# A four-layer convolution chain: the first spectral layer's rows back along w, moved into the work on both sides of their stage

## The chip, the cores and the metric

The kernel runs on one core of a Trainium2 chip. The metric is the device time of one execution in microseconds, as a median of several runs. Of the kernel before, three runs gave 3878.82, 3879.38 and 3880.02 us, a median of 3879.38 us. The profile is of one execution with a span of 3876.6 us, and all times in the trace count from the start of that span.

## The reference

The input is an image of 48 x 48 positions with 768 channels in float32. Four layers follow each other: an attention block with an MLP (layer 0), a spectral layer (1), a scan (2) and a second spectral layer (3). The change touches the end of layer 1 and the beginning of layer 2.

```
# layer 1 (and 3): FFT over h and w, a small complex MLP on 8 blocks of 96 channels, FFT back, plus x
xs = fft2(x) over (h, w), half of w kept: 25 columns
o1 = relu(xs @ w1 + b1); o2 = o1 @ w2 + b2          # complex, by blocks
x = irfft2(softshrink(o2)) + x
# layer 2: projections of every position, then 12 steps of a diffusion
B, C = silu(x @ W_B + ..), silu(x @ W_C + ..)       # 256 wide each
X, alpha, theta, gamma = x @ W_X, W_dec, W_th, W_lam # 4, 64, 32 and 1 wide
for i in range(12):
    inj = rope(B, theta * (i + 1)) * X
    H = alpha * depthwise3x3(H) + (1 - gamma) * alpha * prev + gamma * inj
```

The inverse FFT is done in two parts: back along h, and then back along w. The second part is what this study calls the rows back.

## The kernel before

The spectrum of layer 1 lies in DRAM in two tensors, `yu[0]` and `yu[1]`, for the two halves of 384 channels each. `spectrum_mix` reads it in items: for each half (first 1, then 0), each group of 5 columns of the spectrum and each block of 96 channels. An item goes through four stages: FFT along h (`s_fft_h`, L1420), first layer (`s_mlp1`, L1434 to L1445), second layer and softshrink (`s_mlp2`, L1455 to L1461), and FFT back along h (`s_ifft_h`, L1470 to L1477). The stages are staggered over steps: in one step the FFT of item i stands beside the last stage of item i - 4. After 40 items there are four more steps that only drain what is under way. A group of 5 columns is stored to `yu` when its four blocks are done. After each step a hook is called (`beside(step)`); in the kernel before it makes the last forward FFT rows in steps 1 and 4, and loads the scan's weights `wsc` in step 8.

Then the rows back (`afno_first`, L1549 to L1558). For each half and each of 6 groups of 8 image rows, `load_spectrum` reads a tile `gt` of 672 KB from `yu` (three buffers). For each of three tiles of 128 channels, four products with `gt` as weights (100 x 128) and the small matrix `iw` (100 x 96) as moving operand fill 384 columns of a PSUM bank, which `Evac` copies in turn on ScalarE (L57) and VectorE (L59) into `x2T`, the whole image with channels on partitions. That is 144 products and 36 copies.

Then the scan (`scan_phase`). Its left-side tiles are set up (memsets on GpSimd, L1045 and L1047; four PSUM tiles `pss` of two banks, cleared on VectorE, L1043). The projections (L1082) run over 24 tiles of two image rows. A tile takes 12 products of 112 positions: six for 357 columns and six for 256, one for each 128 channels of x. VectorE adds the bias while it empties the two banks (L1084). Three tiles make a q, and for each of 8 q a chain on VectorE and ScalarE follows: silu, sigmoid, sines and cosines for the rope, and the start values of the recurrence (`H`, `s0`, `s1`). Then the steps of the diffusion begin (L1172 on).

The order of instructions on each engine is not that of the source. A scheduler places them by its own costs and by what they depend on, so instructions of different stages are interleaved where their data allows it. At run time each engine runs its own list in order, and waits at an instruction whose semaphores are not yet there. DMAs of these stages are issued from one queue (SP), in order too.

Of the kernel before, what the change touches and what calls it, by code (L numbers as in the profile page):

```python
# [2 lines left out]

# [8 lines left out]
F32 = mybir.dt.float32  # L12
# [7 lines left out]
P = 128  # L20
G = 48
T = G * G
C = 768
NC = C // P
NT = T // P
NH, HD = 12, 64
FF = 4 * C
NF = FF // P
TB = 384
NTB = T // TB  # L30
# [6 lines left out]
NB, BS = 8, 96  # L37
KW = G // 2 + 1
KC = 5
YR = 112  # L40
NKC = KW // KC
# [955 lines left out]
    return r, a  # L997


def scan_phase(tc, ident, w, w_close, wts, xT, xT_close, c_d, cr_d, out_open):  # L1000

# [18 lines left out]
    with tc.tile_pool(name="sc_s", bufs=1, side="left") as sp:  # L1022
# [9 lines left out]
        with (  # L1032
# [6 lines left out]
            bands0 = stp.tile([P, GC, 4, G], F32, tag="bands0", name="bands0")  # L1039
            nc.sync.dma_start(bands0, bands_d[:, :GC])  # L1040
            pss = [pm.tile([P, 2, 512], F32, tag=f"c{i}", name=f"c{i}") for i in range(4)]
            for ps in pss:
                V.memset(ps, 0.0)  # L1043
            top = slice(96, P)
            GP.memset(H, 0.0)  # L1045
# [2 lines left out]
            with (  # L1048
# [10 lines left out]
                def temp(shape, tag, q, bufs=1):  # L1059
                    return tp.tile([P, *shape], F32, tag=tag, name=f"{tag}_{q}", bufs=bufs)[:K]  # L1060
# [8 lines left out]
                def over_r(v, n):  # L1069
                    return v.unsqueeze(2).to_broadcast([K, n, RR, R4])  # L1070

                for q in range(NQ):
                    prs = slice(q * R4, (q + 1) * R4)
                    za = temp([NA, R4], "za", q, 2)
                    g = temp([NCR, R4], "g", q, 2)
                    for t in range(R4):
                        tok = (q * R4 + t) * P
                        ps = pss[(q * R4 + t) % 4]
                        parts = ((za, 0, NA), (g, NA, NCR))
                        for i, (z, c0, n) in enumerate(parts):  # L1080
                            for cc in range(NC):
                                nc.tensor.matmul(ps[:K, i, :n], lhsT=xT[:, cc, tok : tok + K], rhs=w[:, cc, c0 : c0 + n], start=cc == 0, stop=cc == NC - 1)  # L1082
                        for i, (z, c0, n) in enumerate(parts):
                            V.tensor_tensor(z[:, :, t], ps[:K, i, :n], bias[:K, c0 : c0 + n], ALU.add)  # L1084
                    g3 = g.rearrange("p (n r) t -> p n r t", r=RR)
                    c, x = za[:, :NCR, :], za[:, NA - 1 - RR : NA - 1, :]
                    thz = za[:, NCR + NN : NCR + NN + NM, :]
                    alq = al[:K, :, prs]
                    ga = temp([1, R4], "ga", q)
                    for t in (g, x):  # L1090
                        nc.scalar.activation(t, t, AF.Silu)
                    th = temp([NM * R4], "th", q)
                    V.tensor_copy(th, thz.rearrange("p m t -> p (m t)"))
                    cs = sincos(th, q, "t1")
                    V.tensor_scalar(th, th, float(ITERS), None, ALU.mult)
                    cs12 = sincos(th, q, "t12")
                    nc.scalar.activation(c, c, AF.Silu)
                    nc.scalar.activation(ga, za[:, NA - 1 : NA, :], AF.Sigmoid)
                    nc.scalar.activation(alq, za[:, NCR : NCR + NN, :], AF.Sigmoid)
                    nc.sync.dma_start(c_d[:K, q, :NCR], c)  # L1100
                    nc.sync.dma_start(c_d[:K, q, NCR:].rearrange("p (s m) t -> p s m t", s=2), cs12)
                    c1q = c1[:K, :, prs]
                    V.tensor_scalar(c1q, cs[:, 0], 2.0, None, ALU.mult)

                    def by_gamma(out, in_):
                        for t in range(R4):
                            nc.scalar.mul(out[:, :, t], in_[:, :, t], ga[:, 0, t : t + 1])


                    om = temp([1, R4], "om", q)  # L1110
                    V.tensor_scalar(om, ga, -1.0, 1.0, ALU.mult, ALU.add)
                    be = temp([NN, R4], "be", q)
                    V.tensor_tensor(be, alq, om.to_broadcast([K, NN, R4]), ALU.mult)
                    bc = temp([NN, R4], "bc", q)
                    gc = temp([NM, R4], "gc", q)
                    V.tensor_tensor(gc, c1q, ga.to_broadcast([K, NM, R4]), ALU.mult)
                    for j in range(2):
                        ms = slice(j * NM, (j + 1) * NM)
                        V.tensor_tensor(bc[:, ms], be[:, ms], gc, ALU.add)
                    ac = temp([NN, R4], "ac", q)  # L1120
                    V.tensor_tensor(ac, alq, cb[:K].unsqueeze(2).to_broadcast([K, NN, R4]), ALU.mult)

                    V.tensor_tensor(g.rearrange("p (n r) t -> p n (r t)", r=RR), g.rearrange("p (n r) t -> p n (r t)", r=RR), x.rearrange("p r t -> p (r t)").unsqueeze(1).to_broadcast([K, NN, RR * R4]), ALU.mult)
                    i0 = temp([NCR, R4], "i0", q)
                    i03 = i0.rearrange("p (n r) t -> p n r t", r=RR)
                    m = [temp([NM, RR, R4], f"m{j}", q) for j in range(2)]
                    for op in turn(V, i0, g, over_r(cs[:, 0], NM), over_r(cs[:, 1], NM), m):
                        op()

                    V.tensor_tensor(H[:K, :, :, 1 + q * R4 : 1 + (q + 1) * R4], i03, over_r(ac, NN), ALU.add)  # L1130
                    flat = lambda v: v.rearrange("p n r t -> p (n r) t")

                    u = temp([NCR, R4], "u", q)
                    by_gamma(u, i0)
                    t0 = s0[:K, :, :, prs]
                    V.tensor_tensor(t0, g3, over_r(be, NN), ALU.mult)
                    V.tensor_tensor(flat(t0), flat(t0), u, ALU.add)
                    u = temp([NCR, R4], "u", f"{q}_1")
                    by_gamma(u, g)
                    t1 = s1[:K, :, :, prs]  # L1140
                    V.tensor_tensor(t1, i03, over_r(bc, NN), ALU.mult)
                    V.tensor_tensor(flat(t1), flat(t1), u, ALU.subtract)  # L1142
            w_close()
            xT_close()
            wo, bo = out_weights()
            with (
                tc.tile_pool(name="sc_h", bufs=1, side="right") as hp,
# [115 lines left out]
def block_kernel(ctx: ExitStack, tc: tile.TileContext, a: dict):  # L1263
# [41 lines left out]
    def opened(name, shape, side):  # L1305
        stack = ExitStack()
        pool = stack.enter_context(tc.tile_pool(name=name, bufs=1, side=side))
        return pool.tile(shape, F32, tag=name, name=name), stack.close
# [21 lines left out]
    follow_in = lambda *args: afno_follow(nc, xa_d, a["fw2"], yu, todo, *args)  # L1330
    mlp_phase(tc, ident, w1s_d, a["mlp_b1"], a["mlp_w2"], w2s_d, a["mlp_b2"], a["ln2_g"], a["ln2_b"], xr_d, xa_d, follow_in)

    x2T, x2T_close = opened("x2T", [P, NC, G * HD], "right")
    wsc, wsc_close = opened("wsc", [P, NC, a["W_scan"].shape[1]], "right")
    afno_first(tc, a, yu, x2T, follow_in, lambda: nc.sync.dma_start(wsc, a["W_scan"].rearrange("(c p) n -> p c n", p=P)))

    closes = []

# [5 lines left out]
    wts = [a[k] for k in ("b_scan", "bias_scan", "conv_b", "bands", "W_out", "b_out")]  # L1344
    c_d = dram.tile([P, 8, NN * RR + 2 * NM, 3], F32, tag="c_d", name="c_d")
    cr_d = dram.tile([P, 8, NN * RR, 3], F32, tag="cr_d", name="cr_d")
    x3 = scan_phase(tc, ident, wsc, wsc_close, wts, x2T, x2T_close, c_d, cr_d, out_open)
    afno_second(tc, a, x3, yu)
    for close in reversed(closes):
        close()  # L1350
# [138 lines left out]
def load_spectrum(nc, pool, yu, half, g, name, bufs):  # L1489
    gt = pool.tile([YR, 4, TB], F32, tag="gt", name=f"{name}_gt_{half}_{g}", bufs=bufs)  # L1490
    nc.sync.dma_start(gt, yu[half][:, 4 * g : 4 * g + 4, :])
    return gt
# [33 lines left out]
    return follow  # L1526


def afno_first(tc, a, yu, x2T, follow_in, load_next):

    nc = tc.nc
    ev = Evac(nc)
    x2v = x2T.rearrange("p c (h w) -> p c h w", w=HD)
    nc.gpsimd.memset(x2v[:, :, :, G:], 0.0)
    with (
        tc.tile_pool(name="f1_g", bufs=1, side="right") as gp,  # L1540
        tc.tile_pool(name="f1_p", bufs=8, space=PSUM) as pm,
    ):

        def psum(tag):
            return pm.tile([P, 512], F32, tag="m", name=f"f1_{tag}")

        iw = gp.tile([4 * KW, BS], F32, tag="iw", name="f1_iw")
        follow = follow_in(gp, 1)
        spectrum_mix(tc, "f1", a, "L1", yu, psum, True, "left", (1, 0), lambda step: follow(psum) if step in (1, 4) else load_next() if step == 8 else None)  # L1549
        nc.sync.dma_start(iw, a["iw"])  # L1550
        for half in (1, 0):
            for g in range(NTB):
                gt = load_spectrum(nc, gp, yu, half, g, "f1", 3)
                for ct in range(NC // 2):
                    ps = psum(f"w_{half}_{g}_{ct}")
                    for i in range(4):
                        nc.tensor.matmul(ps[:, i * BS : (i + 1) * BS], lhsT=gt[: 4 * KW, i, ct * P : (ct + 1) * P], rhs=iw, start=True, stop=True)
                    ev(x2v[:, half * NC // 2 + ct, 8 * g : 8 * g + 8, :G], ps[:, :TB].rearrange("p (h w) -> p h w", w=G))  # L1558


def afno_second(tc, a, x3, yu):
# [145 lines left out]
```

## Time and profile before

| stretch | from, us | to, us | what TensorE does |
|---|---|---|---|
| spectrum mix, layer 1 | 2850 | 3049.3 | f_x, f_o, f_z, f_u; clock 1.00 from 2866 to 3049 |
| rows back along w | 3049.3 | 3110.5 | f_w, 144 products |
| wait for the first bank | 3110.5 | 3112.5 | nothing |
| projections of the scan | 3112.5 | 3264.1 | c, 288 products |
| rest of the chain of the last q | 3264.1 | 3275.6 | nothing |
| diffusion steps | 3275.6 | 3519 | c from H and bands |

In the profile, the page's first part gives each engine's busy time. A line of a list of stretches has the stretch, its length, then for each engine the busy time and in parentheses the number of records, the granted clock of TensorE as a share of full speed, the busy share of the DMA engines and their rate. A product of float32 operands shows as two records of weight load and two of matmul. In the lines of single instructions, the brackets say how long the engine was idle before and what ended that.

### The profile page before, as it was taken

Reading aid. Unit: us, or ns where it says so; the run is one execution under the profiler, and the core shown is the slowest. Engines: PE = TensorE matmul, PEld = TensorE weight load, DVE = VectorE, ACT = ScalarE, POOL = GpSimd, SP = SyncE. Lnnn points to the kernel's source line nnn. Section 1 sums busy time; section 2 is a strip of 40 time slices with the busy share of each in tenths; the row PEclk is TensorE's granted clock in tenths of the full one; section 3 lists DMA queues with packets and bytes.
Section 4 is the critical chain, followed back from the end, with each engine's and each line's share of the span. In section 5 each row is a group of like instructions: output and inputs, shape, how many; then the busy total and the mean of one; then the engine's idle time right before and its main releaser. Section 6 shows DMA issues by size and latency. Waiting matters only on the chain. (4 is left out here: it accounts for less than half of the span.)

```text
span 3876.6 us, 54460 instructions
## 1 busy us (share of the span) xinstructions
PE 3761.5 (97%) x22018; PEld 2285.7 (59%) x22018; DVE 2059.0 (53%) x3185; ACT 1141.9 (29%) x1907; POOL 658.4 (17%) x496
## 2 busy tenths in 40 slices
PE   8999989999999999998999999999999998999998
PEld 4666544444444444455555555555568866996685
DVE  6655456666666666555425333232335367995355
ACT  1322244444444444421310120021023246223341
POOL 3101011111111111024000000000023301981131
PEclk9999989999999999999999999999999799999999
DMA  7656563424232322134334434433454302110444
GB/s 257 210 187 197 173 183 112 127 92 133 84 110 83 105 87 76 36 95 161 123 105 155 150 107 124 147 122 108 132 139 110 96 24 93 40 32 22 146 108 159
DMA packets 266810, 460.43 MB, mean 119 GB/s; under 512 B 32989, under 2 KB 219349, under 8 KB 260055
## 3 DMA queue, kind: packets, MB, share of 16 engines
q1 hardware_dynamic: 256919, 436.23, 36.3%
q10 hardware_dynamic: 9632, 20.65, 1.4%
q8 instruction: 175, 2.87, 0.3%
q14 instruction: 84, 0.69, 0.1%
HBM read 318.49 MB, written 138.31 MB: 118 GB/s over the span
## 5 line engine op out<-in xcount | busy, mean ns | idle before, releaser
L576 DVE TENSOR_TENSOR acc<-acc,p 128x768 f32<-128x768 f32 x576 | 582.8, 1012 | 354.9 <-ACT p L568 316.5
L568 ACT ACTIVATE p<-s 128x768 f32<-128x768 f32 x648 | 478.5, 812 | 692.7 <-PE s L566 580.5
L929 PE MATMUL p<-w,h 128*128 128x384 f32 x1512 | 492.7, 486 | 0.0
L558 PE MATMUL s<-qt,kv 64*128 64x384 f32 x2592 | 478.5, 501 | 9.1 <-ACT p L568 7.4
L587 PE MATMUL av<-p,kv 128*64 128x384 f32 x2592 | 464.5, 493 | 0.0
L929 PEld LDWEIGHTS p<-w,h 128*128 128x128 f32 x1512 | 286.1, 190 | 196.9
L558 PEld LDWEIGHTS s<-qt,kv 64*128 64x128 f32 x2592 | 233.1, 187 | 249.9 <-ACT p L568 116.0
L587 PEld LDWEIGHTS av<-p,kv 128*64 128x64 f32 x2592 | 170.0, 136 | 225.2 <-issue 215.8
L866 PE MATMUL p<-x2nT,w 128*128 128x384 f32 x864 | 294.0, 490 | 3.1 <-issue 3.1
L294 PE MATMUL qk<-xnT,wqk 128*128 128x384 f32 x756 | 252.5, 491 | 5.2 <-DMA wqk<-wqk_d 5.2
L1172 PE MATMUL c<-H,bands 128*48 128x96 f32 x5632 | 242.8, 247 | 12.1 <-issue 11.5
L566 PE MATMUL s<-bt,oneh 120*128 120x384 bf16 x1296 | 248.3, 328 | 0.0
L1172 PEld LDWEIGHTS c<-H,bands 128*48 128x48 f32 x5632 | 234.2, 123 | 20.9 <-issue 11.9
L866 PEld LDWEIGHTS p<-x2nT,w 128*128 128x128 f32 x864 | 165.4, 192 | 119.1 <-issue 6.0
L866 PE MATMUL p<-xT,w 128*128 128x384 f32 x648 | 220.8, 486 | 0.0
L566 PEld LDWEIGHTS <-oneh 120*128 120x128 bf16 x1296 | 109.1, 98 | 174.3 <-issue 115.1
L294 PEld LDWEIGHTS qk<-xnT,wqk 128*128 128x128 f32 x756 | 144.6, 193 | 99.9 <-issue 8.5
L905 POOL TENSOR_TENSOR rr<-rr,ml_b 128x1152 f32<-128x1152 f32 x12 | 33.5, 2788 | 954.4 <-DMA rr<-xr_d 660.8
L861 ACT ACTIVATE h<-h,ml_b 128x384 f32<-128x384 f32 x144 | 88.3, 614 | 346.6 <-DVE h L881 174.3
L1180 POOL TENSOR_TENSOR t<-s,c 128x768 f32<-128x768 f32 x80 | 144.8, 1836 | 214.3 <-DVE s L1142 203.8
L866 PEld LDWEIGHTS p<-xT,w 128*128 128x128 f32 x648 | 123.1, 190 | 85.9
L1082 PE MATMUL c<-wsc,x2T 128*112 128x357 f32 (+1 forms) x576 | 151.6, 426 | 2.0 <-DVE c L1043 2.0
(314 smaller groups left out, 4778.7 us busy)
## 6 DMA issues: line engine op xcount, KB each, us to landing
w<-w1s_d SPq DMA_DIRECT2D x36, 768.0 KB
w<-w2s_d SPq DMA_DIRECT2D x36, 768.0 KB
bt<-rh_d SPq DMA_DIRECT2D x144, 162.0 KB
w<-w1s_d SPq DMA_DIRECT2D x36, 576.0 KB
w<-in_mlp_w_dram SPq DMA_DIRECT2D x27, 768.0 KB
wqk<-wqk_d SPq DMA_DIRECT2D x12, 1344.0 KB
yu<-f_ys SPq DMA_DIRECT2D x24, 672.0 KB
f_gt<-yu SPq DMA_DIRECT2D x24, 672.0 KB
```

Source lines behind the costliest of these rows:

```text
L294: nc.tensor.matmul(p[:, :TB], lhsT=w[:, n, c, :], rhs=ops[sb][n][:, c, :], start=c == 0, stop=c == NC2 - 1)
L558: nc.tensor.matmul(ps[:, s, :QB], lhsT=keys[pr % 2][rows, kt * P : (kt + 1) * P], rhs=qbs[qc % 2][0][rows], start=True, stop=False)
L566: nc.tensor.matmul(ps[:, s, :QB], lhsT=oneh[:NBR, b % 3, :], rhs=qbs[qc % 2][1][:NBR, s, b // 3, j, :], start=False, stop=True)
L568: nc.scalar.activation(p, ps[:, :, :QB], AF.Exp)
L576: nc.vector.tensor_tensor(probs[c], probs[c], p, ALU.add)
L587: nc.tensor.matmul(avs[c][rows, :QB], lhsT=vals[pr % 2][:, kt, rows], rhs=p[:, s, :], start=kt == 0, stop=kt == NT - 1)
L861: nc.scalar.activation(h, h, AF.Gelu, bias=b1c[:, k : k + 1])
L866: nc.tensor.matmul(p[:, :TB], lhsT=w[n][:, c, :], rhs=rhs[n][:, c, :], start=c == 0, stop=c == NC2 - 1)
L929: nc.tensor.matmul(ps[t][:, :TB], lhsT=hs[left, f][:, t * P : (t + 1) * P], rhs=wt[:, f % KW2, :], start=f == 0, stop=f == NF2 - 1)
L1082: nc.tensor.matmul(ps[:K, i, :n], lhsT=xT[:, cc, tok : tok + K], rhs=w[:, cc, c0 : c0 + n], start=cc == 0, stop=cc == NC - 1)
L1172: nc.tensor.matmul(ps[r0 : r0 + G, k // 4, cols], lhsT=bands[:, n - GC, i, :] if gr else bands0[:, n, i, :], rhs=H[:, n, :, d : d + NPR], ...
L1180: GP.tensor_tensor(t, sc[:, ch], c1[:, m0 : m0 + GC].unsqueeze(2).to_broadcast([P, GC, RR, NPR]), ALU.mult)
```

## The change

The rows back lose their stage. Those of half 1, whose spectrum is complete when the mix turns to half 0, are made beside the last items: tiles of `gt` are loaded in four of the last steps, one group of 8 image rows follows each of the four draining steps, and two more come after them. They go into `xh`, which holds only this half of the channels. Those of half 0 are made inside the scan's projections: group 0 ahead of the first tile, and each further group two tiles ahead of the four tiles that read it. They go into one of two small homes (`x2_0`, `x2_1`), each for 8 image rows. For these products the fourth of the PSUM tiles is used, one bank for each group of 384 columns in turn, so the projections have three tiles in place of four. A projection sums the six channel tiles in reversed order, so that those from `xh` come first.

The tiles `gt` (now four buffers), `iw` and the two homes lie in a pool that lives until the projections end. The loads of the scan's biases find room earlier; the scheduler puts them, and the sum of the two biases, into the early mix. `gc` shares the buffer of `th`. The purpose is to take a stage away in which only one kind of work is done, and to lay its work beside others.

```diff
 def scan_phase(...)
-            for ps in pss:
+            for ps in pss[:3]:
                 V.memset(ps, 0.0)
...
+                turn_of = itertools.cycle(range(2))
+                banks = lambda tag: pss[3][:, next(turn_of), :]
+                xs = [rows_back(0, banks)]
                 for q in range(NQ):
...
                     for t in range(R4):
-                        tok = (q * R4 + t) * P
-                        ps = pss[(q * R4 + t) % 4]
+                        pr = q * R4 + t
+                        if pr % 4 == 2 and pr + 4 < NPR:
+                            xs.append(rows_back(pr // 4 + 1, banks))
+                        x_of = lambda cc: (xs[pr // 4], cc, pr % 4 * P) if cc < NC // 2 else (xh, cc - NC // 2, pr * P)
+                        ps = pss[pr % 3]
...
-                            for cc in range(NC):
-                                nc.tensor.matmul(ps[:K, i, :n], lhsT=xT[:, cc, tok : tok + K], rhs=w[:, cc, c0 : c0 + n], start=cc == 0, stop=cc == NC - 1)
+                            for cc in reversed(range(NC)):
+                                v, c, tok = x_of(cc)
+                                nc.tensor.matmul(ps[:K, i, :n], lhsT=v[:, c, tok : tok + K], rhs=w[:, cc, c0 : c0 + n], start=cc == NC - 1, stop=cc == 0)
...
-                    gc = temp([NM, R4], "gc", q)
+                    gc = temp([NM * R4], "th", f"{q}_g").rearrange("p (m t) -> p m t", t=R4)
 def afno_first(...)
+    iw = rp.tile([4 * KW, BS], F32, tag="iw", name="f1_iw")
+    homes = [rp.tile([P, HC, 8 * HD], F32, tag=f"x2{i}", name=f"x2_{i}") for i in range(2)]
...
+    def load(half, g):
+        gts[half, g] = load_spectrum(nc, rp, yu, half, g, "f1", 4)
+
+    def back(half, g, dst, psum):
+        gt = gts.pop((half, g))
+        for ct in range(HC):
+            ps = psum(f"w_{half}_{g}_{ct}")
+            for i in range(4):
+                nc.tensor.matmul(ps[:, i * BS : (i + 1) * BS], lhsT=gt[: 4 * KW, i, ct * P : (ct + 1) * P], rhs=iw, start=True, stop=True)
+            ev(in_rows(dst)[:, ct, :, :G], ps[:, :TB].rearrange("p (h w) -> p h w", w=G))
...
-        nc.sync.dma_start(iw, a["iw"])
-        for half in (1, 0):
-            for g in range(NTB):
-                gt = load_spectrum(nc, gp, yu, half, g, "f1", 3)
-                for ct in range(NC // 2):
-                    ps = psum(f"w_{half}_{g}_{ct}")
-                    for i in range(4):
-                        nc.tensor.matmul(ps[:, i * BS : (i + 1) * BS], lhsT=gt[: 4 * KW, i, ct * P : (ct + 1) * P], rhs=iw, start=True, stop=True)
-                    ev(x2v[:, half * NC // 2 + ct, 8 * g : 8 * g + 8, :G], ps[:, :TB].rearrange("p (h w) -> p h w", w=G))
+        def first_back(g):
+            back(1, g, xh[:, :, 8 * g * HD : 8 * (g + 1) * HD], psum)
+            if g + 4 < NTB:
+                load(1, g + 4)
+
+        def beside(step):
+            last = 2 * NKC * (NB // 2)
...
+            elif last - 12 <= step < last - 4 and step % 2 == 0:
+                load(1, (step - last + 12) // 2)
+            elif step >= last:
+                first_back(step - last)
+
+        spectrum_mix(tc, "f1", a, "L1", yu, psum, True, "left", (1, 0), beside)
+        for g in range(4, NTB):
+            first_back(g)
+            load(0, g - 4)
+
+    def rows_back(g, banks):
+        if g + 2 < NTB:
+            load(0, g + 2)
+        back(0, g, homes[g % 2], banks)
+        return homes[g % 2]
```

More of the change, by code (lines that the diff above doesn't have):

```diff
@@ L1 @@
+import itertools
 import math
@@ L997, in reduce_angle, with scan_phase @@
     return r, a
-def scan_phase(tc, ident, w, w_close, wts, xT, xT_close, c_d, cr_d, out_open):
+def scan_phase(tc, ident, w, wts, rows_back, xh, x_close, c_d, cr_d, out_open):
     nc = tc.nc
@@ L1142, in scan_phase @@
                     V.tensor_tensor(flat(t1), flat(t1), u, ALU.subtract)
-            w_close()
-            xT_close()
+            x_close()
             wo, bo = out_weights()
@@ L1331, in block_kernel @@
     mlp_phase(tc, ident, w1s_d, a["mlp_b1"], a["mlp_w2"], w2s_d, a["mlp_b2"], a["ln2_g"], a["ln2_b"], xr_d, xa_d, follow_in)
-    x2T, x2T_close = opened("x2T", [P, NC, G * HD], "right")
+    xh, xh_close = opened("xh", [P, NC // 2, G * HD], "right")
     wsc, wsc_close = opened("wsc", [P, NC, a["W_scan"].shape[1]], "right")
-    afno_first(tc, a, yu, x2T, follow_in, lambda: nc.sync.dma_start(wsc, a["W_scan"].rearrange("(c p) n -> p c n", p=P)))
+    rp_stack = ExitStack()
+    rp = rp_stack.enter_context(tc.tile_pool(name="f1_w", bufs=1, side="right"))
+    rows_back = afno_first(tc, a, yu, xh, rp, follow_in, lambda: nc.sync.dma_start(wsc, a["W_scan"].rearrange("(c p) n -> p c n", p=P)))
     closes = []
@@ L1346, in block_kernel, with x_close @@
     cr_d = dram.tile([P, 8, NN * RR, 3], F32, tag="cr_d", name="cr_d")
-    x3 = scan_phase(tc, ident, wsc, wsc_close, wts, x2T, x2T_close, c_d, cr_d, out_open)
+    def x_close():
+        rp_stack.close()
+        wsc_close()
+        xh_close()
+    x3 = scan_phase(tc, ident, wsc, wts, rows_back, xh, x_close, c_d, cr_d, out_open)
     afno_second(tc, a, x3, yu)
@@ L1526, in afno_follow, with afno_first @@
     return follow
-def afno_first(tc, a, yu, x2T, follow_in, load_next):
+def afno_first(tc, a, yu, xh, rp, follow_in, load_next):
     nc = tc.nc
     ev = Evac(nc)
-    x2v = x2T.rearrange("p c (h w) -> p c h w", w=HD)
-    nc.gpsimd.memset(x2v[:, :, :, G:], 0.0)
+    HC = NC // 2
+    iw = rp.tile([4 * KW, BS], F32, tag="iw", name="f1_iw")
+    homes = [rp.tile([P, HC, 8 * HD], F32, tag=f"x2{i}", name=f"x2_{i}") for i in range(2)]
+    in_rows = lambda v: v.rearrange("p c (h w) -> p c h w", w=HD)
+    for v in (xh, *homes):
+        nc.gpsimd.memset(in_rows(v)[:, :, :, G:], 0.0)
+    gts = {}
+    def load(half, g):
[7 more added lines that the diff above has]
+            ev(in_rows(dst)[:, ct, :, :G], ps[:, :TB].rearrange("p (h w) -> p h w", w=G))
     with (
-        tc.tile_pool(name="f1_g", bufs=1, side="right") as gp,
+        tc.tile_pool(name="f1_f", bufs=1, side="right") as fp,
         tc.tile_pool(name="f1_p", bufs=8, space=PSUM) as pm,
@@ L1545, in psum @@
             return pm.tile([P, 512], F32, tag="m", name=f"f1_{tag}")
-        iw = gp.tile([4 * KW, BS], F32, tag="iw", name="f1_iw")
-        follow = follow_in(gp, 1)
-        spectrum_mix(tc, "f1", a, "L1", yu, psum, True, "left", (1, 0), lambda step: follow(psum) if step in (1, 4) else load_next() if step == 8 else None)
-        nc.sync.dma_start(iw, a["iw"])
-        for half in (1, 0):
-            for g in range(NTB):
-                gt = load_spectrum(nc, gp, yu, half, g, "f1", 3)
-                for ct in range(NC // 2):
-                    ps = psum(f"w_{half}_{g}_{ct}")
-                    for i in range(4):
-                        nc.tensor.matmul(ps[:, i * BS : (i + 1) * BS], lhsT=gt[: 4 * KW, i, ct * P : (ct + 1) * P], rhs=iw, start=True, stop=True)
-                    ev(x2v[:, half * NC // 2 + ct, 8 * g : 8 * g + 8, :G], ps[:, :TB].rearrange("p (h w) -> p h w", w=G))
+        follow = follow_in(fp, 1)
+        def first_back(g):
[4 more added lines that the diff above has]
+            last = 2 * NKC * (NB // 2)
+            if step in (1, 4):
+                follow(psum)
+            elif step == 8:
+                nc.sync.dma_start(iw, a["iw"])
+                load_next()
+            elif last - 12 <= step < last - 4 and step % 2 == 0:
[11 more added lines that the diff above has]
+        return homes[g % 2]
+    return rows_back
 def afno_second(tc, a, x3, yu):
```

## The prediction

> **What bounds the kernel now.** I read the page's engine line first, then the mean granted TensorE clock, then the span in stretches around the edited stage, then the waits there, then single instructions.
>
> ```profile
> PE 3761.5 (97%) x22018; PEld 2285.7 (59%) x22018; DVE 2059.0 (53%) x3185; ACT 1141.9 (29%) x1907; POOL 658.4 (17%) x496
> ...
> PEclk9999989999999999999999999999999799999999
> ```
>
> TensorE is busy 97% of the span, so time comes back only where it does less work, idles less, or does the same work at a higher clock. The one low digit of the clock row (7) is the slice that holds the edited stage.
>
> ```profile
> core 0: us, PE busy (x) PEld busy (x) DVE busy (x) ACT busy (x) POOL busy (x), PEclk, DMA share, GB/s
> 3040.00:3050.00 10.00, 7.04 (x52) 5.33 (x53) 5.02 (x9) 0.88 (x2) 0.81 (x1) 0.99 0.01 2
> 3050.00:3110.00 60.00, 60.00 (x283) 60.00 (x283) 9.64 (x18) 9.33 (x19) 23.19 (x6) 0.50 0.44 129
> 3112.00:3118.00 6.00, 5.53 (x10) 2.99 (x11) 3.86 (x5) 0.00 (x0) 0.00 (x0) 0.50 0.43 92
> 3120.00:3160.00 40.00, 40.00 (x157) 27.43 (x156) 23.91 (x69) 18.00 (x32) 0.00 (x0) 1.00 0.07 21
> 3160.00:3200.00 40.00, 40.00 (x155) 27.12 (x155) 32.42 (x84) 27.63 (x48) 0.00 (x0) 1.00 0.08 24
> 3200.00:3260.00 60.00, 60.00 (x234) 41.02 (x233) 48.85 (x124) 38.09 (x65) 0.00 (x0) 1.00 0.07 22
> ```
>
> The rows back along w (L1557) fill 60 us in which TensorE never idles, yet its clock is granted at 0.50 throughout; DVE and ACT are 16% busy. The scan's projections (L1082) follow at full clock after some 6 us at half, TensorE full, DVE 81%.
>
> ```profile
> L1557 PE MATMUL f_w<-f_iw,f_gt x288: 247/421/422, 3049.3 to 3110.0; 100*128 100x96 f32 x144
> ...
> PE c L1082 <- DVE c L1043: 2.0, 1, 2.0
> ...
> 3046.42 0.33 PE L1455 MATMUL f_z<-f_w,f_o 97*96 97x96 f32 x2
> 3046.59 0.33 PE L1456 MATMUL f_z<-f_w,f_o 97*96 97x96 f32 x2
> 3048.45 1.02 PE L1470 MATMUL f_u<-f_Z,f_ih 96*96 96x480 f32 x2 [1.53 <-DVE f_Z L1461]
> 3049.30 2.06 PE L1557 MATMUL f_w<-f_iw,f_gt 100*128 100x96 f32 x11
> ```
>
> 144 products (two records each) take 3049.3 to 3110.5: 0.42 us each. Just before, TensorE drains the last items of the mix: it waits for DVE's clip and subtract (1.53 us here, 1.43 us one item earlier), and at about 3049.9 the clock halves. After the rows it waits 2.0 us for the memset of the first projection bank (L1043).
>
> [...] 60 us of this stream did not lift the half clock, while the projections did in 5.5 us. [...] Here POOL's memset, waiting for the last store of the mix (issued at 3050.18), starts at 3054.67: 4.5 us for 720 KB[...].
>
> **The change part by part.** All from a common point: 3039.8, when TensorE ends the last first-layer product of the mix (L1436); the projections end at 3264.05. That is 224.2 us before.
>
> *Rows of half 1 into the drain.* The changed program puts 12 products behind each draining step and the last 36 behind the final f_u. TensorE's work there: 72 x 0.213 = 15.3 us, three f_u of 0.8 us, 20 f_z of 0.17 us (starts in the timeline), 21.1 us in sum. The DVE waits go: between z and its u now lie 12 products, 2.6 us, more than the 1.5 us waited. Their tiles come early (before, the first load of half 1 was issued at 2964.9). The end moves to 3060.9. The price 0.213 lies between 0.17 (f_z, no wider than its weight load) and 0.42 (half clock); I take 0.213 as half of 0.42.
>
> *The gap to the projections.* DVE still clears the first bank after the last copy: 2.0 us kept. One of four memsets goes, but not the one waited for. Start at 3062.9.
>
> *First tile of half 0.* Its load waits for the mix's last store. The last f_u ends about 3053.4, its add 0.9 us later, the store 4.5 us after that, then about 4.6 us for 672 KB (estimate from that store): 3063.4. TensorE asks for it after three projection products (1.8 us), at 3064.7. Hidden by 1.3 us; if not, a few us.
>
> *Projections.* Before: 151.6 us, of which about 5.5 us at half clock, so 148.8 us at full. Added: 72 x 0.213 = 15.3 us, 164.1 together. Evictions added: 9 ACT copies of 0.48 and 9 DVE copies of 0.56, 5 us on DVE, which has 19% idle: hidden. Three banks in place of four: a bank is wanted again 12 us after its product ended, while DVE drains within 1 to 2 us in the timeline: nothing.
>
> *New waits.* The order of the changed program shows each three groups of a tile waiting for the copy of the group before, all in one PSUM tile, so its two banks don't overlap. Queued behind such a wait are TensorE's projections, in order. Other projection products stand between, so most waits are met; but for tile 2 the first copy stands on ACT behind the scaling u of the previous q. In the first q that ends 11.2 us after the q's last product (3134.0 to 3145.2), the copy 0.5 later; TensorE arrives 10.7 us after. About 1 us; eight such points from tile 2 on: 0 to 10 us, I take 3.
>
> *Clock.* Before, projections start half-clocked and lose 2.8 us. After, [...] 0 to 3 us, I take 1.5.
>
> *At no cost.* Bias loads and their add (0.8 us of DVE) move into the early mix, where DVE is 57% busy; the load of the second bias follows a store issued at 2876.7 and is wanted about 2883.8, 7 us later. gc shares th's buffer, whose readers are done. POOL's 24 us of memsets start at about 3059 and end near 3083; the first write into what they clear comes at about 3090. The tail after the projections (16.5 us) has a fifth ACT table load of 1.28 us in the last q, ahead of sin but with al earlier: H comes out the same within 0.5 us.
>
> Sum: 3062.9 + 164.1 + 3 + 1.5 = 3231.5, against 3264.05: 32.5 us. 3879.4 - 32.5 = **3847 us**.
>
> **Rivals.**
> *Half clock follows the rows.* If the stream can't hold the clock, the last 36 products of the drain cost 7.6 us more, the projections start cold (+1.5 over my mean), and some groups amid them too: some 10 us, 3857. For: 60 us without rising. Against: [...] a stretch with TensorE 56% busy (2848.0 to 2851.4) kept the full clock.
> *Waits on copies.* If in each of tiles 2 to 5 two groups wait 3 us more for DVE or ACT, mid-chain: 24 us, minus my 3, 3868. Against: DVE and ACT have 3.5 us more room per q than before, and TensorE never waited there.
> *Slower.* Groups wait the whole 13 us DVE chain of a q less one 6 us product, 7 us x 8, minus my 3: 3900. Only if the order fits the chip badly; DVE's bank evictions in the trace come within 1 us, against it.
> *No change.* The scan's start is bound elsewhere (memsets, loads of bands): the memsets end 10 us before they are wanted, against it.
>
> **How the numbers follow.** Forecast 0.63, half clock 0.15, waits 0.13, slower 0.05, no change 0.04. With no stall and no cold start the sum gives 3842.5; densities slightly better than taken, 3839. Upwards, the range takes the half-clock case and the nearer part of the waits: 3863. Faster by over 0.2% (below 3871.6): 0.91; same 0.04; slower 0.05.
>
> **What would show it.** Drain rows at 0.21 us with clock 1.00 and the last f_u near 3053; projections from about 3063 to 3231; L1572's copies waited for by TensorE a few us at most. Wrong if the clock row shows 0.5 in the drain, if TensorE idles over 10 us in the projections, or if the first tile of half 0 lands after 3065.

## The result, and the profile after

The changed kernel takes 3846.73 us (median of 4 runs, 3843.78 to 3847.93) against 3879.1 us before (4 runs, 3878.42 to 3880.02): a ratio of 0.9915, with a 95% interval from 0.9898 to 0.9932, or 32.4 us less. The forecast was 3847 us, between 3839 and 3863.

The profiled execution has a span of 3846.1 us. First the two lines of the page, engine totals and clock row:

```profile
PE 3731.5 (97%) x22018; PEld 2255.8 (59%) x22018; DVE 2057.4 (53%) x3184; ACT 1143.0 (30%) x1908; POOL 654.5 (17%) x498
...
PEclk9999989999999999999999999999999999999999
```

TensorE runs the same 22018 records, in 30.0 us less of busy time, and its share of the span is still 97%. So it does the same products faster, and rests only a little less (the table below has that part). The 7 in the clock row is gone.

The same list of stretches as before, around the places where the rows now stand (TensorE, its weight loads, DVE, ACT, POOL, then clock, DMA share, GB/s):

```profile
3040.00:3050.00 10.00, 10.00 (x91) 9.04 (x91) 4.77 (x9) 2.20 (x5) 0.81 (x1) 1.00 0.38 106
3050.00:3060.00 10.00, 10.00 (x88) 9.54 (x86) 4.34 (x8) 2.40 (x5) 1.17 (x1) 1.00 0.44 117
3060.00:3064.00 4.00, 1.99 (x16) 1.85 (x15) 2.25 (x4) 0.48 (x1) 4.00 (x1) 0.90 0.94 269
3064.00:3068.00 4.00, 4.00 (x15) 2.50 (x15) 1.45 (x2) 0.00 (x0) 3.94 (x4) 0.68 1.03 296
3120.00:3160.00 40.00, 39.90 (x177) 28.58 (x178) 29.51 (x76) 22.45 (x40) 0.00 (x0) 1.00 0.07 20
```

The drain, at whose end the clock fell to 0.50 before, has it at 1.00 with TensorE full (20.00 of 20.00 us). Only after the gap of 2.01 us ahead of the projections is it lower: 0.59, 0.50, 0.50 and 0.70 in the four stretches of 1 us from 3063, and 1.00 in the next. In the projections the clock is 1.00 with the rows among them, in every stretch taken from 3067 to 3230.

The rows' line in this kernel is L1572. Its two groups (rows of half 1, written to `f_w`; rows of half 0, written to a bank of `c`), and then single instructions:

```profile
L1572 PE MATMUL f_w<-f_iw,f_gt x144: 247/275/275, 3039.6 to 3061.3; 100*128 100x96 f32 x144
L1572 PE MATMUL c<-f_iw,f_gt x144: 246/275/350, 3066.9 to 3199.7; 100*128 100x96 f32 x144
```
```profile
3052.61 0.97 PE L1487 MATMUL f_u<-f_Z,f_ih 96*96 96x480 f32 x2
3053.42 8.18 PE L1572 MATMUL f_w<-f_iw,f_gt 100*128 100x96 f32 x72
3063.61 3.51 PE L1092 MATMUL c<-wsc,xh 128*112 128x357 f32 x6 [2.01 <-DVE c L1045]
3066.95 1.03 PE L1572 MATMUL c<-f_iw,f_gt 100*128 100x96 f32 x8
...
3244.13 18.08 PE L1181 MATMUL c<-H,bands 128*48 128x96 f32 x394 [12.35 <-issue]
```

The median record is 275 ns in place of 421. From start to start a product takes 0.22 us (8 records, four products, in the 0.87 us from 3066.95 to 3067.82, where the next projection starts) in place of 0.42. The last f_u starts at 3052.61 without a wait, where before it waited 1.53 us. The first rows of half 0 follow the third projection with no idle time in brackets: their tile had landed. The first diffusion step starts at 3244.13, before at 3275.56.

Where the time came from, measured from the end of the mix's last first-layer product (3039.8 before, 3039.6 after) to the end of the projections (3264.05 and 3231.77), 32.1 us in sum:

| term | before, us | after, us | gain, us |
|---|---|---|---|
| 144 products of the rows | 61.2 (3049.3 to 3110.5) | 15.9 + 15.7 | 29.6 |
| rest of the drain, with its waits | 9.5 | 6.1 | 3.4 |
| gap before the projections | 2.0 | 2.0 | 0 |
| lost to a cold start of the projections | 2.8 | 1.5 | 1.3 |
| waits of the rows for copies | 0 | about 2.4 | -2.4 |

15.9 is 72 products at 0.221 us (24 records in 2.65 us), 6.1 the remainder of the drain's 22.0, and 15.7 is 72 at 0.218. The missing 0.2 is in the two values for the projections alone, 148.8 and 148.6. The 2.4 is what remains of the projections' 168.2 us after 148.6 us for 288 products at full clock (0.60 and 0.432 us each, from the timeline), 15.7 and 1.5. Nine tenths of the gain is the clock. The 3.4 us of the drain is another kind of gain: before, TensorE waited there for VectorE (0.22, 1.43 and 1.53 us), and now rows fill these waits. No other work is hidden, for TensorE is full in the rows and in the projections on both sides.

### The profile page after: what moved, and what is told of

The parts are those of the page before. It is cut to its first block, busy times and chain, and to the rows that moved or that the text cites. A ratio compares the mean times of both kernels' runs of the same rounds, so it can differ in the third digit from the quotient of the medians.

```text
span 3846.1 us, 54463 instructions
## 1 busy us (share of the span) xinstructions
PE 3731.5 (97%) x22018; PEld 2255.8 (59%) x22018; DVE 2057.4 (53%) x3184; ACT 1143.0 (30%) x1908; POOL 654.5 (17%) x498
## 5 line engine op out<-in xcount | busy, mean ns | idle before, releaser
L1181 PEld LDWEIGHTS c<-H,bands 128*48 128x48 f32 x5632 | 234.4, 123 | 21.7 <-issue 12.7
L597 DVE RECIPROCAL rec<-rs 128x384 f32<-128x384 f32 x36 | 92.1, 2558 | 99.6 <-PE rs L595 99.6
```

The lines of the kernel that those rows point to most:

```text
L597: nc.vector.reciprocal(rec, rs[:, :QB])
L1181: nc.tensor.matmul(ps[r0 : r0 + G, k // 4, cols], lhsT=bands[:, n - GC, i, :] if gr else bands0[:, n, i, :], rhs=H[:, n, :, d : d + NPR], ...
```

## The experiments

Theory A: the 144 products hold a full clock but can't raise one, so that in a stage entered at half clock they take 60 us, and entered at full clock 31 us. Rivals: the products are slow for their stage (their tiles, their copies); the move gains by laying the rows beside other work or in waits (Theory B in the expectations); where the rows stand among the projections matters.

**e2, half 1 in the drain only.** From the kernel before, both halves still outside the projections:

```diff
+            elif last - 12 <= step < last - 6 and step % 2 == 0:
+                load(1, (step - last + 12) // 2)
+            elif step >= last:
+                next_back(step - last)
...
+        for i in range(4, len(order)):
+            next_back(i)
```

> One part alone: the rows of half 1 go into the drain as in the change, those of half 0 stay a stage of their own behind them, projections as before. Theory A: half 1 at full clock (15.3 us for 30.3, and the drain's waits filled). Half 0 must wait for the store of the last item, some 2 us of idleness after 3061.6, as long as the wait in which the changed kernel lost its clock: if the clock falls there, half 0 runs at 0.42 us a product and the time is about 3863; if it holds, about 3847. Theory B expects the saving in proportion to the rows laid beside other work, about half of 32 us: 3863 too, but with the clock at 1.00 in half 0's stage, so the clock row decides.

Measured: 3862.62 us (3860.39 to 3863.81), ratio 0.9959 (0.9945 to 0.9973), against 3878.28 us before. The stretches of its trace, and then the products of half 0:

```profile
3050.00:3060.00 10.00, 8.73 (x74) 8.20 (x72) 3.44 (x6) 2.34 (x5) 2.56 (x1) 1.00 0.67 187
3060.00:3064.00 4.00, 1.20 (x6) 1.23 (x6) 0.00 (x0) 0.00 (x0) 3.94 (x2) 0.61 1.01 284
3064.00:3080.00 16.00, 16.00 (x77) 16.00 (x76) 2.23 (x4) 2.39 (x5) 16.00 (x5) 0.50 0.62 173
```
```profile
3062.80 31.01 PE L1559 MATMUL f_w<-f_iw,f_gt 100*128 100x96 f32 x144 [4.07 <-DMA f_gt<-yu]
```

Half 1 runs at full clock. Then TensorE waits 4.1 us for the first tile of half 0 (the expectation said some 2 us), the clock goes to 0.50, and products of the same form, with tiles and copies of the same size, take nearly twice as long (0.43 us each) while TensorE is 16.00 of 16.00 us busy. Theory B had the same time, but with the clock at 1.00.

**e3, half 0 in the projections only.** From the changed kernel, with half 1 in a stage after an unfilled drain:

```diff
-            elif step >= last:
-                first_back(step - last)
...
-        for g in range(4, NTB):
+        for g in range(NTB):
             first_back(g)
-            load(0, g - 4)
+        load(0, 0)
+        load(0, 1)
```

> The other part alone: the rows of half 1 stay a stage of their own behind an unfilled drain, those of half 0 go into the projections as in the change. Theory A: the clock halves at the end of the drain as before and half 1's 72 products take 30.3 us; half 0 costs 15.3 us at full clock plus some 4 us of waits: about 3866 us. If the rows in the projections were the part that loses (waits on copies), 3875 or more; if they were hidden, as laying beside other work would promise, 3850.

Measured: 3862.42 us (3861.44 to 3867.66), ratio 0.9962 (0.9948 to 0.9976). The expectation was 3866. In its trace, of the slowest of the five runs, half 1 runs at half clock (0.50 from 3052 on). Half 0 (written to `c`) runs at full clock, except its first two groups, which still find the half clock that half 1 left (0.50 up to 3084, 1.00 from 3088):

```profile
L1572 PE MATMUL f_w<-f_iw,f_gt x144: 247/421/422, 3048.3 to 3077.9; 100*128 100x96 f32 x144
...
L1572 PE MATMUL c<-f_iw,f_gt x144: 246/275/527, 3079.0 to 3217.6; 100*128 100x96 f32 x144
```

The two parts give 15.7 and 15.9 us, together the 32 of the whole: each half gains by itself, and mostly by the clock (72 times about 0.2 us is some 14 us). In e2 the waits of the drain are filled too, but the new wait of 4.1 us takes that back.

**e1, the drain filled, the rows left where they were.** Twelve unread products behind each of three draining steps, so that the stage is entered at full clock; nothing of the computation is left out.

```diff
+            elif step >= 40 and step < 43:
+                for ct in range(3):
+                    ps = psum(f"fill_{step}_{ct}")
+                    for i in range(4):
+                        nc.tensor.matmul(ps[:, i * BS : (i + 1) * BS], lhsT=w[0][:, i, ct * P : (ct + 1) * P], rhs=w[0][:, 5, :BS], start=True, stop=True)
```

> The kernel before, whose rows back stay a stage of their own; only the three waits of the drain are filled: 12 products of 128 x 128 with 96 columns, which nothing reads, are put behind each of the first three draining steps. Theory A (the gain is the clock alone: the stream of rows can hold the full clock but not raise it): the stage keeps 1.00 and takes 144 x 0.213 = 30.7 us in place of 61, less about 3 us for the drain being longer, so about 3850 us; if the loads of the tiles, three buffers deep, can't follow at twice the pace, up to 3858. Theory B (the gain of the change comes from laying the rows beside other work): about 3879 or a little more. Theory C [...]: half clock again inside the stage, 3865 or more.

Measured: a median of 3875.97 us, ratio 0.9982 (0.997 to 0.9994). By its median this is not the 3850 of Theory A but where Theory C (the stream lets the clock fall by itself) put it, at 3865 or more. The median hides two groups, though: of 20 runs six took 3852.8 to 3862.5 us and fourteen 3869.5 to 3880.7, and the mean granted clock goes with it (0.984 to 0.986, and 0.978 to 0.982). The profiled execution was one of the first group. In it the stage (L1574) has 275 ns per record, and the clock is 1.00 all through:

```profile
3063.00:3073.00 10.00, 9.38 (x85) 9.25 (x84) 2.79 (x5) 2.39 (x5) 9.94 (x5) 1.00 0.82 218
```
```profile
PE f_w L1574 <- DMA f_gt<-yu: 1.6, 3, 0.7
```

So the stage as such is not slow: entered at full clock it took 34.6 us, with three waits for tiles, the longest of 0.7 us. This refutes the rival of the stage. But the time and the clock of the other fourteen runs say that they lost the full clock, and that needed a cause. None of those fourteen was profiled.

**e7, a burst ahead of the stage.** No filling; six products of 512 columns right before the rows, unread too.

```diff
+        ps = psum("burst")
+        for i in range(6):
+            nc.tensor.matmul(ps, lhsT=w[0][:, i % 6, :P], rhs=w[0][:, 5, :512], start=True, stop=True)
         nc.sync.dma_start(iw, a["iw"])
```

> The kernel before, rows in a stage of their own as there, with six unread products of 128x128 by 512 columns put between the drain's last product and the stage; they leave nothing out and write a buffer nobody reads. Theory A (the stage's products can hold a full clock but not raise it): the burst costs 6 products, three or so at 1.7 us while the clock is half and the rest at 0.85, about 7.7 us (estimated from 0.595 us for 357 columns at full clock); the 144 products then take 30.5 us in place of 60: 3879 - 29.5 + 7.7 = about 3857, where small waits do not let it fall. Rival (the clock in this stage is held down by the products' own form in a stage without other work, or falls at once): 60 us as before, 3879 + 7.7 = 3887.

Measured: 3854.93 us, ratio 0.9939 (0.9925 to 0.9953); four runs at 3851.8 to 3856.0 and one at 3870.76. That one was profiled, which shows the fall itself. The timeline of TensorE, and then 1 us stretches, two in the burst and four around the late tile:

```profile
3047.43 6.29 PE L1564 MATMUL f_burst<-wsc 128*128 128x512 f32 x12
3053.56 13.54 PE L1572 MATMUL f_w<-f_iw,f_gt 100*128 100x96 f32 x120
3068.22 34.62 PE L1572 MATMUL f_w<-f_iw,f_gt 100*128 100x96 f32 x168 [1.13 <-DMA f_gt<-yu]
```
```profile
3048.00:3049.00 1.00, 1.00 (x2) 0.34 (x1) 0.32 (x1) 0.00 (x0) 0.00 (x0) 0.50 0.00 0
3050.00:3051.00 1.00, 1.00 (x4) 0.39 (x3) 0.00 (x0) 0.00 (x0) 0.00 (x0) 1.00 0.96 250
...
3067.00:3068.00 1.00, 0.09 (x1) 0.00 (x0) 0.00 (x0) 0.48 (x1) 1.00 (x1) 1.00 1.02 276
3068.00:3069.00 1.00, 0.78 (x7) 0.81 (x8) 0.00 (x0) 0.00 (x0) 1.00 (x1) 1.00 1.00 191
3069.00:3070.00 1.00, 1.00 (x10) 1.00 (x10) 0.56 (x1) 0.00 (x0) 1.00 (x1) 0.94 1.00 301
3070.00:3071.00 1.00, 1.00 (x6) 1.00 (x6) 0.00 (x0) 0.48 (x1) 1.00 (x2) 0.50 0.82 227
```

In the burst the clock rose from 0.50 to 1.00, and 60 products ran at 0.226 us each. One tile came 1.13 us late. About 1.7 us after that wait the clock fell, and the last 84 products took 0.412 us each in the mean, TensorE full to the end of the stage; in some 33 us the clock never rose again. The wait cost 1.13 us itself, and what followed some 16 us (84 times 0.186). One trace shows that the fall came after the wait, not that the wait made it; the next two runs try that.

**e8, the burst with early loads**, and **e9, the filled drain with early loads.** Each has four buffers for the tiles in place of three and the first four tiles loaded within the last items, so that no product waits for a tile.

```diff
+            elif 28 <= step < 36 and step % 2 == 0:
+                g = (step - 28) // 2
+                pre[1, g] = load_spectrum(nc, gp, yu, 1, g, "f1", 4)
...
-                gt = load_spectrum(nc, gp, yu, half, g, "f1", 3)
+                gt = pre.pop((half, g), None) or load_spectrum(nc, gp, yu, half, g, "f1", 4)
```

> The previous kernel with four buffers for the spectrum's tiles in place of three and the first four tiles of half 1 loaded within the drain's items (steps 28, 30, 32 and 34, as in the change), so that no product of the stage waits for a tile. Theory A with the rider that waits for tiles are what dropped the clock in most runs of the filled drain: 3857 as for the previous kernel, but the same in every run, within 0.1%; the previous kernel may scatter up to 3887. Rival (the fall is chance in the clock itself, not waits): the scatter is as wide here.

> The filled drain (twelve unread products behind each of three draining steps, rows in their own stage) with four buffers for the spectrum's tiles and the first four tiles loaded within the last items, as in the kernel with the burst and early loads. If waits for tiles are what dropped the clock in 14 of 20 runs of the filled drain: all runs at 3850 to 3858, the rows at clock 1.00. If the fall comes by chance while the stream runs without a wait: two groups again, most runs at 3873 to 3881.

Measured: e8 3854.24 us (five runs, 3849.89 to 3856.77), ratio 0.9941 (0.9927 to 0.9955); e9 3855.83 us (five runs, 3853.2 to 3862.02), ratio 0.9944 (0.993 to 0.9957). None of the ten falls into the upper group, though one run of e9, at 3862.02, lies above the 3850 to 3858 that were expected. In e8's trace the 144 products are one unbroken line, at 0.224 us each, and in e9's too:

```profile
3053.28 32.30 PE L1575 MATMUL f_w<-f_iw,f_gt 100*128 100x96 f32 x288
```
```profile
3052.21 32.30 PE L1577 MATMUL f_w<-f_iw,f_gt 100*128 100x96 f32 x288
```

Of the filled drain's runs fourteen of twenty were in the upper group with three buffers, none of five with four buffers and early loads. So the fall went with the late tiles: if the stream alone made it (Theory C), or chance, it would have shown in e9 as often as in e1. e8 says less on this, as e7 had only one run of five in the upper group; and in e8's profiled run the clock had not fallen ahead of the burst, so that e7's trace alone shows it rising in a burst. The spread was narrow but not within the 0.1% expected of e8: 0.18%, and 0.23% in e9. And e8 and e9 have the rows in a stage of their own, with unread work added, and still keep 23.7 and 21.7 us of the 32. The burst itself takes 5.2 us in e8's trace (3048.1 to 3053.3); with it, 28.9 us, near the 29.6 of the table. That settles what most of the change's gain comes from: not where the rows stand, but the clock they are run at.

**e4, separate buffers for the rows in the projections.** In the changed kernel the two banks for the rows are halves of one PSUM tile. Here they are two tiles; the fourth tile of two banks is made after the projections.

```diff
-                turn_of = itertools.cycle(range(2))
-                banks = lambda tag: pss[3][:, next(turn_of), :]
+                rbs = itertools.cycle([rb.tile([P, 512], F32, tag=f"r{i}", name=f"r{i}") for i in range(2)])
+                banks = lambda tag: next(rbs)
```

> The changed kernel, but the two banks of the rows in the projections are two PSUM tiles of their own, so that a group of products needn't wait for the copy of the group just before; the fourth tile of the diffusion is made from them afterwards. If the 4.5 us that TensorE waits for these copies are a cost of the serial tile, they go: 3842 to 3843 us, against 3846.7. If the copies are late because ScalarE and VectorE are in their chains, a third group still waits for the first: 3845 to 3847.

Measured: 3844.42 us (3841.64 to 3846.22), ratio 0.9913 (0.9897 to 0.993). The main waits of the rows (total us, times, longest), first the changed kernel's, then e4's:

```profile
PEld c L1572 <- ACT x L58: 3.2, 5, 0.9
```
```profile
PEld r L1576 <- DVE x L60: 0.8, 1, 0.8
```

Most waits for the copy of the group before are gone from the trace: over the rows' lines, TensorE and its weight loads together, 4.0 us (3.2, 0.5 and 0.3) fall to 1.0 (0.8 and 0.2). These records overlap in part, so they are not 3.0 us of time; what the stage gained is worked out below, 1.0 to 1.2 us. The medians differ by 2.3 us, or by 1.5 us when each is taken against the kernel before as timed beside it. The intervals overlap: the time doesn't separate the two kernels.

**e5, the clearing later**, and **e6, both edits.** In e5 VectorE clears the three tiles after their last use in the projections, not ahead of them.

```diff
-            for ps in pss[:3]:
-                V.memset(ps, 0.0)
...
+                        if pr + 3 >= NPR:
+                            V.memset(ps, 0.0)
```

> The changed kernel with the clearing of the three two-bank buffers moved from the head of the scan's stage to behind the last use of each in the projections, so nothing but the data stands between the drain's last product and the first projection. The clearing itself still runs, later. Theory A (the 2.0 us gap at 3061.6 is the wait for that clearing, and it is what lets the clock fall to 0.50 for about 4 us): gap gone (-2.0) and no cold start (-1.4): 3843.3 against 3846.7. Rival (the gap's end was only named by the clearing, and another wait ends at nearly the same time, or the cold start comes back at the next wait for a copy): -0.5 or less, 3846.2 to 3846.7.

> The previous edit together with separate one-bank buffers for the rows in the projections (run before alone at 3844.4, ratio 0.9913). Theory A: the two gains add, since they are waits at different places of a TensorE that is full elsewhere: 3844.4 - 3.4 = 3841.0, and less if the clearing of the fourth buffer, made only after the projections, falls on the way (+0.5). Rival (they are the same few microseconds of slack): 3843.3 to 3844.4.

Measured: e5 3843.05 us (3841.87 to 3844.2), ratio 0.991 (0.9895 to 0.9925); e6 3843.16 us (3840.28 to 3844.0), ratio 0.9912 (0.9899 to 0.9926). e5's first projection:

```profile
3061.03 3.23 PE L1090 MATMUL c<-wsc,xh 128*112 128x357 f32 x10 [0.74 <-DVE xh L60]
```

The gap is 0.74 us, now the wait for the last copy into `xh`, and no 2 us stretch of the projections is below full clock. So the clearing was the wait, and with a gap of 0.74 us in place of 2.01 the cold start is gone, as it is in e6's trace with the same gap. In the medians e6 is no faster than e5, which is what the rival said; the time cannot decide it, and the traces below do.

e6 was then timed beside the changed kernel on one chip:

> The changed kernel itself, beside the next one on the same chip: 3846 to 3847, ratio 0.9915.

> Separate buffers and later clearing once more, beside the changed kernel on the same chip. Theory A: faster than it by the waits and cold start that its trace no longer shows, some 5 us of TensorE time, of which the first measurement gave 3.6 us; 3841 to 3844. Rival: the difference was one between chips, and both measure the same within 1 us.

Measured: changed kernel 3846.23 us (3840.54 to 3848.48), ratio 0.9916 (0.9902 to 0.993); e6 3842.8 us (3840.51 to 3845.18), ratio 0.991 (0.9894 to 0.9925). e6 is 3.4 us faster in the medians, as in the first measurement (3.6), but the runs overlap, so the time does not separate them.

The traces do, if the stage alone is measured: from the start of the first row product in the drain to the first diffusion step. First two lines of the changed kernel, timed again, and then two of e6, timed again:

```profile
3035.74 2.81 PE L1572 MATMUL f_w<-f_iw,f_gt 100*128 100x96 f32 x24
3240.46 21.77 PE L1181 MATMUL c<-H,bands 128*48 128x96 f32 x479 [12.36 <-issue]
```
```profile
3038.03 2.81 PE L1576 MATMUL f_w<-f_iw,f_gt 100*128 100x96 f32 x24
3239.16 23.04 PE L1185 MATMUL c<-H,bands 128*48 128x96 f32 x506 [12.90 <-issue]
```

| trace | first row product, us | first diffusion step, us | stage, us |
|---|---|---|---|
| changed kernel | 3039.59 | 3244.13 | 204.5 |
| changed kernel again | 3035.74 | 3240.46 | 204.7 |
| e4, separate buffers | 3037.38 | 3240.93 | 203.6 |
| e5, clearing later | 3038.28 | 3240.59 | 202.3 |
| e6, both | 3039.22 | 3240.31 | 201.1 |
| e6 again | 3038.03 | 3239.16 | 201.1 |

Two executions of the same kernel agree here within 0.2 us. e4 gains 1.0 to 1.2 us, e5 2.2 to 2.4 and both together 3.4 to 3.6: the two gains add, as Theory A had it. e5's part can be told: 1.3 us less gap and 1.5 us of cold start gone, less 0.5 us that TensorE idles longer ahead of the first diffusion step (12.90 us in place of 12.35). The whole time hides all this. The profiled executions of the changed kernel again and of e6 again have the same span, 3838.7 us, since the rest of the program took 3634.0 us in one and 3637.6 us in the other.

## Why the prediction was right

Point by point, by its own steps:

- *The stream can hold the clock.* This was the disputed step, with 0.15 on its failure; before the change the rows had 1.00 for no more than their first 0.6 us (3049.3 to about 3049.9), so that it could hold was the author's estimate. The trace agrees (clock 1.00 in 3040 to 3060), and e1, e7, e8 and e9 show it apart from the change. It is right with a condition the prediction didn't see: in e7 the clock went from 1.00 to 0.50 some 1.7 us after a wait of 1.13 us, and the rows that followed, some 33 us of them, were not seen to bring it back. Other products beside the rows were not needed while nothing waited: e8 and e9 have 1.00 over the 32.3 us of the rows in a stage of their own. Beside the projections the clock was seen to recover: in the changed kernel it drops to 0.50 after the gap of 2.01 us too, and it is back by 3067, with projections running from 3063.61. Of the prediction's arguments against the half clock, the stretch from 2848.0 to 2851.4 has TensorE 59% busy in the trace (2.01 of 3.40 us, clock 1.00), not 56%.
- *Rows of half 1 in the drain*: 21.1 us forecast, 22.0 measured (3039.6 to 3061.6). A product takes 0.221 us, not the 0.213 that was taken as half of 0.42, and 72 of them make 0.6 of the difference; the rest is in the tail of the last one.
- *The gap*: 2.0 us forecast, 2.01 measured, ended by the clearing, as e5 shows.
- *First tile of half 0*: no wait was measured. Its load was issued at 3058.65, near the time that the forecast's 3063.4 minus 4.6 us implies, but TensorE asked at 3066.95 instead of 3064.7: by the later start and the cold clock there was more time than thought. When the tile landed isn't in the trace, so whether it was before the 3065 of the prediction's signs stays open.
- *Projections*: 168.6 us forecast with waits and cold start, 168.2 measured. The waits for copies cost some 2.4 us (3 forecast). The cause is in part as foreseen: with two PSUM tiles in place of one, e4's stage is 1.0 to 1.2 us shorter, some half of the 2.4; what stays has no cause shown beyond e4's wait of 0.8 us for a copy on VectorE. The forecast had eight such waits, for copies late on ScalarE; in the changed kernel the rows' weight loads show six, five for ScalarE and one for VectorE, none over 0.9 us. The cold start cost 1.5 us, as taken: the first three projections take 3.34 us from start to start in place of 1.80.
- *Tail*: 12.35 us idle before the first diffusion step against 11.51, 0.8 us more where "within 0.5" was said. (The forecast's 16.5 us for this tail doesn't fit the trace, which has 11.5 before the change; the sum doesn't use it.) The fifth table load of the forecast stands on ScalarE in this stretch (1.28 us, from 3239.57); that it makes the 0.8 wasn't tried.
- *The rivals*: half clock did not follow the rows; waits on copies stayed near the forecast; DVE's chain never held the rows up for long; a bound elsewhere is excluded by e2 and e3, each of which moved the end by its own part.

Where luck had a share: 3847 lies 0.3 us from the median, closer than the runs lie to each other (3843.78 to 3847.93). The terms of the stage missed by up to 0.9 us, in both directions; up to the end of the projections the traces show 32.1 us where 32.5 was forecast, and the slower tail takes 0.8 us of it. And had one of the drain's tiles come a microsecond late, as in e7's profiled run, the products after it could have cost 0.19 us more each, some 7 us for the last 36 (an estimate from e7's 0.412 and 0.226 us, not tried). The prediction used the early loads to remove a wait; their larger use was to protect the clock. The chance given to half clock was right to be there.

In the kernel before, the rows from 3050 to 3110 had TensorE 60.00 of 60.00 us busy, and the clock stayed at 0.50: TensorE's busy time in the profile isn't by itself what raises the clock.

## What to carry to other kernels

Read the clock beside the busy time: here an engine 97% busy ran a stage of 60 us at clock 0.50, and the signs were one digit of the clock row, and products that took nearly twice as long from start to start as the same form took elsewhere (0.42 against 0.22 us; the single records were 421 against 275 ns). This stream of small products with a fresh weight load each kept 1.00 over 32.3 us where it found it and never waited (e8, e9), and stayed at 0.50 over 60 us where it found that (the kernel before). For a stream like it, try to enter it at full clock, to load its tiles early enough that it never waits, or to lay it beside products under which the clock was seen to come back, as under the projections here. And when overlapping a stage pays, ask which of its costs fell; here nine tenths (29.6 of 32.1 us) was not hidden work, but the same work done faster.

## What was not expected of the hardware

In e7 one late tile of 1.13 us was followed by some 33 us of half clock under a full TensorE, which cost some 16 us. In these traces the length of a wait alone doesn't tell whether the clock falls. In the filled drain three waits of up to 0.7 us left the clock at 1.00. After the gap of 2.0 us before the projections it was at 0.50 in the changed kernel; in e8 and e9, where the same stage of rows runs up to that same gap, e8's trace has 1.00 all through and e9's has the fall:

```profile
3085.00:3090.00 5.00, 2.99 (x14) 1.92 (x13) 3.55 (x6) 1.48 (x2) 4.31 (x1) 1.00 0.66 215
```
```profile
3087.00:3089.00 2.00, 2.00 (x4) 0.93 (x3) 1.68 (x3) 0.00 (x0) 2.00 (x1) 0.50 0.99 400
```

The waits of the drain (1.43 and 1.53 us) stand in e8 as in the kernel before, and e8's trace has the clock at 1.00 through them and through the burst that follows.

What makes the clock fall or rise was not measured. Products of 357 columns (the projections, before 3067 in the changed kernel) and of 512 (the burst, before 3050 in e7) were running when it rose, and so were the mix's own smaller products in the kernel before, with weights of 96 columns and 240 and then 96 columns moving. There it rose some 5 us after their start at 2860.41, between these two stretches:

```profile
2861.00:2865.00 4.00, 4.00 (x20) 3.42 (x19) 0.71 (x2) 1.42 (x4) 0.37 (x1) 0.50 1.03 395
2866.00:2870.00 4.00, 4.00 (x34) 3.28 (x33) 2.24 (x5) 1.68 (x4) 0.60 (x2) 1.00 0.00 0
```

So the clock rose there under products no wider than 240 columns; under the rows, with weights of 128 columns and 96 moving, it was not seen to rise in the 60 us of the kernel before.
